# Pairs of rows in the layer-2 experts, a later channel-mix constant, a shorter router, and identity products in planned holes of a four-layer transformer kernel

## The chip, the core and the metric

The kernel runs on one core of a Trainium2 chip. The core has five engines with a queue each: TensorE (PE in the profile, its weight loads PEld), VectorE (DVE), ScalarE (ACT), GpSimd (POOL) and SyncE (SP, which here only issues DMAs). Every queue runs in program order; engines wait for each other through semaphores. The metric is the device time of one execution in microseconds; all tensors are float32.

## The reference, cut to what matters

Four "macaron" layers work on `x` of shape 4 rows (B) x 512 tokens (S) x 128 features (D). Each layer adds half a feed-forward, an attention, and half a feed-forward again, each on a layer norm of `x`:

```python
x = x + 0.5 * L0_ffn(ln(x));  x = x + L0_attn(ln(x));  x = x + 0.5 * L0_ffn(ln(x))
x = x + 0.5 * L1_ffn(ln(x));  x = x + L1_attn(ln(x));  x = x + 0.5 * L1_ffn(ln(x))
x = x + 0.5 * L2_ffn(ln(x));  x = x + L2_attn(ln(x));  x = x + 0.5 * L2_ffn(ln(x))
x = x + 0.5 * L3_ffn(ln(x));  x = x + L3_attn(ln(x));  x = x + 0.5 * L3_ffn(ln(x))
```

The parts that the change touches are these. The layer-2 feed-forward is a top-1 mixture of 8 experts, per row:

```python
gates = softmax(x @ Wg); expert = argmax(gates); gate = the chosen one's share
pos = running count of the row's tokens of this expert; keep if pos < 512 // 8
y[expert, pos] = gelu(x @ W1[expert]) @ W2[expert]      # W1: 128 x 512, W2: 512 x 128
out[token] = gate * y[expert, pos]                      # zero for tokens over capacity
```

The layer-3 feed-forward mixes each token with the one before it (`mu * x + (1 - mu) * x_prev`) ahead of three products. Layer 0's feed-forward is a top-2 mixture of 8 experts with a shared expert; layer 1's is a low-rank adapter (LoRA) with a gate; layer 1's attention is over the 4 rows at the same token, so row b needs rows 0 to b; the attentions of layers 2 and 3 are 16 heads of 8 features over the row's own tokens, causal in layer 2.

## The kernel before, in words

Layer 0 up to its second routing has an order of its own and is not touched. From the second layer-0 feed-forward to the end everything is one plan, made while the program is built. Each piece of work is a Python generator. It yields a request (`PE(0.95, "psum")`, `DVE(0.7)`, `any_of({...})`: an engine, or a choice of engines, with a cost in microseconds, and the buffers that it needs), and when the request is granted it records the instructions. `run` grants, again and again, the request that can start first; among those that start within `CLOSE` = 0.05 of it, it takes the lowest `RANK`. The table `RANK` holds one number for each process. The order in which requests are granted is the order of every engine's queue, SP's included, so the plan's costs set the order and the chip then runs that order at its own pace. `free` and `took` keep count of buffers in the plan; `clock.done` is the plan's time.

The processes, by name:

- `tile0` to `tile19` (`tiled`): the experts of layer 0's second feed-forward on 128-token tiles. L880 are the up products, L928 transposes, L940 the down products; the results go out by `sorted_y<-ys`.
- `first0` to `first3`: gathers of a row's results (`fetched`, L963 and L972), then the LoRA, attention and LoRA of layer 1 (`l1_row`: `lora`, `l1_attn`). L1364 scales `dT` by the LoRA's gate, which VectorE made (L1554); L1522 is the product after it.
- `heads` (`to_heads`): when all tiles are done it frees the tiles' weights, issues 23 DMAs on SP (L2511) for the weights of layers 2 and 3, calls `l3_others` (L2420: `nmu` = 1 - mu, one VectorE instruction, which reads the transfer issued fourth from the end, `l_mu`), and prepares the two value buffers `V` (L1838, one memset each on GpSimd).
- `send0` to `send7` (`l2_sent`): norm, router, slots of row n % 4 in the first (n < 4) and second mixture; the tokens are scattered to DRAM by four indirect DMAs on GpSimd (L2327).
- `take0` to `take7` (`l2_taken`): the row's 8 x 64 token slots are loaded as `X` (L2345, on SP), transposed (L2351), and go through the experts: 32 up products of 64 columns each (L2366), gelu, 32 down products in pairs that share the array (L2384), and a DMA back.
- `mix0` to `mix7` (`l2_added`): four gathers on GpSimd (L2409) and adds into `x`.
- `begin`, `turning`, `scoring` (L1931), `weighing` (L1947, the exponentials on ScalarE), `masking` (L1959), `values` (L1973), `turned` (L1994), `end`: the attentions of layers 2 and 3, eight "rows" k in order; `channels0` to `channels6`: layer 3's feed-forward; `half0`, `half1`: the last row's end in two halves.

PSUM has three `big` tiles (two banks each) and two `one` tiles in the plan.

Of the kernel before, what the change touches and what calls it, by code (L numbers as in the profile page):

```python
# [17 lines left out]
P = 128  # L18
# [3 lines left out]
NE = 8  # L22
# [18 lines left out]
def done(b):  # L41
# [9 lines left out]
CLOSE = 0.05  # L51
RANK = {
    "begin0": 7.13, "begin1": 16.87, "begin2": 2.08, "begin3": -4, "begin4": 2.25, "begin5": 16.3, "begin6": 18.65, "begin7": 5.19,
    "channels0": 2.52, "channels1": 8.5, "channels2": 0.21, "channels3": -14.23, "channels4": 27.64, "channels5": 35.57, "channels6": 55.73,
    "end0": -14.5, "end1": 16.73, "end2": 9.28, "end3": -13.76, "end4": 20.26, "end5": 8.69, "end6": 7.09, "fetching": 36.35, "first0": 12.23,
    "first1": 12.99, "first2": 13.46, "first3": 15.39, "half0": -16.36, "half1": -8.54, "kept0": 9.26, "looked": 68.09, "looked0": 55.15,
    "looked1": 38.53, "looked2": 55.16, "looked3": 44.23, "looked4": 53.01, "looked5": 64.26, "looked6": 56.59, "masking": 45.18, "mix0": 9.64,
    "mix1": 11.51, "mix2": 7.93, "mix3": -7.76, "mix4": 13.42, "mix5": 20.24, "mix6": 9.63, "mix7": 16.21, "placing": -4.73, "scoring": 23.21,
    "send0": -6.03, "send1": 10.23, "send2": 15.94, "send3": 6.71, "send4": 33.89, "send5": 9.79, "send6": 16.23, "send7": 37.79, "take0": -3.51,
    "take1": -6.11, "take2": 22.65, "take3": 5.52, "take4": 16.36, "take5": 23.51, "take6": 10.29, "take7": 21.36, "tile0": 8.75, "tile1": 6.94,  # L60
    "tile2": 4.64, "tile3": 9.21, "tile4": 1.92, "tile5": 9.1, "tile6": -2.3, "tile7": 4.99, "tile8": 9.81, "tile9": 10.06, "tile10": 10.38,
    "tile11": 10.39, "tile12": 11.4, "tile13": 11.41, "tile14": 11.42, "tile15": 10.69, "tile16": 12.44, "tile17": 12.45, "tile18": 12.46,
    "tile19": 12.87, "turning": 58.41, "values": 43.5, "weighing": 38.58, "whole_l2": 4.79, "whole_l3": 12.44,
}
FETCH = 4.0
DEARER = {"PE": 0.0, "ACT": 0, "DVE": 0.3, "POOL": 0.5, "SP": 0.0}
# [201 lines left out]
def program(ctx: ExitStack, tc: tile.TileContext, a: dict, out: bass.AP, worst):  # L268
# [193 lines left out]
    def by_expert(w, rooms, key):  # L462
# [385 lines left out]
        def tiled(work, iwho):  # L848
# [5 lines left out]
            def unit(u):  # L854
# [28 lines left out]
                yield PE(0.08 + 0.87 * n, "big")  # L883
# [9 lines left out]
                yield PE(0.08 + 0.87 * n, "big", at=t0)  # L893
# [3 lines left out]
                yield DVE(0.58 * n, "us", at=max(clock.done, t2))  # L897
# [15 lines left out]
                yield any_of({"DVE": 0.22 * n, "POOL": 0.1 + 0.35 * n}, at=t2)  # L913
# [498 lines left out]

    def run(procs, calm):

        busy_till = {e: 0.0 for e in ("PE", "DVE", "ACT", "POOL", "SP")}
        clock.on, clock.procs = True, procs
        while procs:
            able = []
            for p in list(procs):
# [30 lines left out]
                if t is not None:  # L1450
                    e = min(r.ways, key=lambda e: max(t, busy_till[e]) + r.ways[e] + DEARER[e])
                    able.append((max(t, busy_till[e]), p.rank, p, kind, e))
# [6 lines left out]
            us = p.req.ways[e]  # L1459
            clock.begun, clock.done, clock.kind, clock.engine = t, t + us + LATENCY, kind, e  # L1460
# [8 lines left out]
    def normal(b, make, kind, ones=False, half=False):  # L1469
# [20 lines left out]
        for h in range(2):  # L1490
            yield any_of({"ACT": 0.97, "DVE": 0.7}, *([kind] if h == 0 else []), at=t0)
            if h == 0:
                took(kind)
                xn = make()
                t1 = clock.done
            for t in (2 * h, 2 * h + 1):
                if clock.engine == "ACT":
                    nc.scalar.activation(xn[:, t, :], x[b][:, t, :], AF.Identity, bias=off[:, t : t + 1], scale=rs[:, t : t + 1])
                else:
                    nc.vector.tensor_scalar(xn[:, t, :], x[b][:, t, :], rs[:, t : t + 1], off[:, t : t + 1], ALU.mult, ALU.add)  # L1500
# [23 lines left out]
    def lora(b, w, work, wait=()):  # L1524
# [20 lines left out]
        yield DVE(0.65, at=t0)  # L1545
# [5 lines left out]
        yield DVE(0.5, at=max(clock.done, t1))  # L1551
# [279 lines left out]
    def heads_at_once(procs, rows, w, work, w3, late):  # L1831
# [5 lines left out]
        for t in V:  # L1837
            nc.gpsimd.memset(t, 1.0)  # L1838
        queries, keys, turns, inverse, through = {}, {}, {}, {}, {}
        sets, us, open_sets = {}, {}, [0, 0]  # L1840
# [33 lines left out]
        def begin(k):  # L1874
# [30 lines left out]
            yield moving(S, wait=[f"valued{k - 2}"] if k > 1 else [])  # L1905
# [3 lines left out]
        def turning():  # L1909
            for k in range(len(rows)):  # L1910
                for g in range(NG):
                    yield any_of({"DVE": 0.46, "ACT": 0.6, "POOL": 0.8}, "qkq", wait=f"q{k}", at=0.0)
                    took("qkq")
                    t = work.tile([P, S], F32, tag="qkq", name="qkq", bufs=2)
                    scaled(t, queries[k], turn[:, g : g + 1])
                    turns[k, g] = t
                    happened(f"turn{k}.{g}")
                    if g == NG - 1:
                        free("q")

        def scoring():
            for i, (k, g, parts, ends) in enumerate(todo):
                yield PE(0.15 + 0.87 * width(parts) / 512, "big", "big", wait=[f"begin{k}", f"turn{k}.{g}"], at=0.0)
# [15 lines left out]
        def weighing():  # L1939
            for i, (k, g, parts, ends) in enumerate(todo):  # L1940
                n = width(parts)
                us[i] = []
                for h in range(NJ // 2):
                    yield ACT(0.1 + 0.87 * n / 512, "pT", wait=f"S{i}", at=0.0)
                    took("pT")
                    p = work.tile([P, 2, S], F32, tag="pT", name="pT", bufs=6)
                    nc.scalar.activation(p[:, :, :n], sets[i][h][:, :, :n], AF.Exp, scale=scale)  # L1947
                    free("big")
                    us[i].append(p)
                    happened(f"E{i}.{h}")  # L1950
# [11 lines left out]
        def values():  # L1962
            po = None
            for i, (k, g, parts, ends) in enumerate(todo):
                first = po is None
                yield PE(0.15 + 0.87 * width(parts) / 512, *(["one"] if first else []), wait=[f"{'M' if rows[k][2] else 'E'}{i}.{h}" for h in range(NJ // 2)], at=0.0)
# [298 lines left out]
    def l2_mixed(w, work, b, rooms, key, late):  # L2265

        sent, kept = [], []
        return l2_sent(w, work, b, rooms, key, sent, kept), l2_taken(w, work, b, rooms, sent, late), l2_added(work, b, rooms, kept, late)

    def l2_sent(w, work, b, rooms, key, sent, kept):  # L2270
# [17 lines left out]
        yield ACT(0.24)  # L2288
        nc.scalar.activation(sh, sh, AF.Exp)
        m, order = little([P, NT, NE], "chosen"), little([P, NT, NE], "order")  # L2290
        gate, best = little([P, NT], "gates"), little([P, NT], "best")
        sofar = little([P, NT - 1, NE], "sofar")
        yield DVE(1.0)
        nc.vector.tensor_reduce(sm, sh, AX.X, ALU.add)
        nc.vector.reciprocal(sm, sm)
        nc.vector.tensor_tensor(sh, sh, wide(sm, NT), ALU.mult)
        nc.vector.tensor_reduce(best, sh, AX.X, ALU.max)
        nc.vector.tensor_scalar(gate, best, 0.5, None, ALU.mult)
        yield DVE(1.4)
        nc.vector.tensor_tensor(order, sh, wide(best, NT), ALU.is_equal)  # L2300
        nc.vector.tensor_tensor(order, order, w["c_first"].unsqueeze(1).to_broadcast([P, NT, NE]), ALU.mult)
# [5 lines left out]
        yield PE(0.5, "psum")  # L2307
        pp, k = spare()
        before = pp[:, : NT * NE].rearrange("p (t e) -> p t e", t=NT)
        l2_counts(before, m, sofar, w)  # L2310
        islot = little([P, NT], "islot", mybir.dt.int32)
        at, place, slot = little([P, NT, NE], "at"), little([P, NT], "place"), little([P, NT], "slot")
        kept += [gate, islot]
        yield DVE(1.4)
# [3 lines left out]
        nc.vector.tensor_tensor(at, m, w["c_slot0"].unsqueeze(1).to_broadcast([P, NT, NE]), ALU.mult)  # L2318
        nc.vector.tensor_reduce(slot, at, AX.X, ALU.add)
# [15 lines left out]
    def l2_taken(w, get, b, rooms, sent, late):  # L2335
# [3 lines left out]
        NH = HID // P  # L2339
        none = NE * CAP  # L2340
        kx, kh, n = ("Xl", "hl", 2) if late else ("X", "h", 1)
        yield ask("PE", 0.0, kx)
        took(kx)
        X = work.tile([P, NT, D], F32, tag="X", name="X", bufs=2 * n)
# [10 lines left out]
        XT = work.tile([P, NE, CAP], F32, tag="X", name="XT", bufs=2 * n)  # L2355
# [4 lines left out]
        for q in range(NE // 2):  # L2360
# [8 lines left out]
            h = work.tile([P, 2, NH, CAP], F32, tag="hr", name="hr", bufs=n * NE // 2)  # L2369
# [4 lines left out]
        yield ACT(2.6 + 2.6)  # L2374
# [3 lines left out]
        for q2 in range(2):  # L2378
# [9 lines left out]
            if q2 == 0:  # L2388
                took(kx)
                y = work.tile([P, NE // 2, D], F32, tag="X", name="y", bufs=2 * n)  # L2390
# [3 lines left out]
        free(kx, clock.done + 2.5)  # L2394

# [27 lines left out]
    def l3_ffn(b, w, get, last, halves=1):  # L2423
# [7 lines left out]
        for m in (1, 0):  # L2431
            yield DVE(1.2, f"t{m}")
# [208 lines left out]
    for kind, n in (("xn", 3), ("X", 2), ("h", 4), ("yg", 4), ("Xl", 4), ("hl", 8), ("ygl", 4), ("cx", 2), ("t0", 1), ("t1", 1), ("kT3", 1), ("r3", 1)):  # L2641
# [17 lines left out]

    def to_heads():  # L2660
# [8 lines left out]
        l3_others(w3, pools[-1])  # L2669
# [3 lines left out]
        yield POOL(3.7)  # L2673
        idle[0] = heads_at_once(procs, rows, wa, work, w3, late)
        for b in range(B):
            procs.append(process(f"channels{b}", l3_ffn(b, w3, late, False), 10 + B + b, [f"mix{B + b}", "change"]))
# [9 lines left out]
    def mixture(n, b, after):  # L2686
        first = n < B
        send, take, add = l2_mixed(w2, (lambda: pools[1]) if first else late, b, row_rooms[b], f"slots{n}", not first)
        procs.append(process(f"send{n}", send, 10 + n, [after]))
        k = n - 1 if first else n - 2  # L2690
        procs.append(process(f"take{n}", take, 10 + n, [f"send{n}", "fetching", "heads"] + ([f"take{k}"] if k >= 0 else []) + ([] if first else ["change"])))
        procs.append(process(f"mix{n}", add, 10 + n, [f"take{n}"] + ([f"mix{n - 1}"] if n else [])))

    for b in range(B):
        mixture(b, b, f"first{b}")
        mixture(B + b, b, f"end{b}")
# [33 lines left out]
```

## Time and profile before

| | us |
|---|---|
| three timed runs, median | 1293.74 |
| lowest, highest of them | 1288.74, 1293.77 |
| the profiled execution, its own time | 1290.51 |
| the profiled execution, its span from first to last instruction | 1288.7 |

| engine | busy us in the span | share |
|---|---|---|
| PE | 1158.0 | 90% |
| DVE | 891.8 | 69% |
| ACT | 707.1 | 55% |
| PEld | 614.1 | 48% |
| POOL | 341.4 | 26% |

The mean granted TensorE clock is 0.958. In the profile's rows a float32 product shows as two matmul records; a transpose by the identity shows as one. A line of a group or of the timeline names the engine, the source line, the tile written and the tile read, and in brackets the idle time of the engine before it and who ended it. "x16" is the number of records merged into one line.

### The profile page before, as it was taken

What the parts mean: (1) busy time and instruction counts of PE and PEld (TensorE: products, weight loads), DVE (VectorE), ACT (ScalarE), POOL (GpSimd) and SP (SyncE); (2) the same over time, 40 slices, a digit from 0 to 9 for tenths busy, and PEclk for the clock granted to TensorE, in tenths of its full rate; (3) what the DMA queues carried; (4) which work ended last, traced back from release to release, by engine and by line L of the source; (5) the groups of instructions that cost most, each with busy time, mean ns of one, the idle gap of its engine ahead of it and who ended that gap; (6) DMA issues with size and microseconds to landing.
All of it is one profiled execution on the core that took longest, in us unless ns stands there. A gap on an engine that the chain in (4) does not pass through costs nothing.

```text
span 1288.7 us, 20383 instructions
## 1 busy us (share of the span) xinstructions
PE 1158.0 (90%) x7066; PEld 614.1 (48%) x7066; DVE 891.8 (69%) x2342; ACT 707.1 (55%) x1030; POOL 341.4 (26%) x323
## 2 busy tenths in 40 slices
PE   5899989999989999997998848798998999999994
PEld 3455544334425335364555426474675665443332
DVE  5697777988988998769668737876637655344233
ACT  2435545654644635442444424466777778778882
POOL 4430223022310400202134535623325233111010
PEclk9899989999999999998999958898999999999998
DMA  8123312111111111101321130001100010000000
GB/s 308 35 72 90 89 57 68 66 60 40 60 62 50 66 50 49 51 1 48 117 66 48 34 109 25 20 16 34 35 25 27 16 34 18 17 25 2 9 9 11
DMA packets 63490, 65.02 MB, mean 50 GB/s; under 512 B 11538, under 2 KB 53907, under 8 KB 62867
## 3 DMA queue, kind: packets, MB, share of 16 engines
q1 hardware_dynamic: 57236, 51.04, 11.8%
q0 software_dynamic: 6144, 12.60, 3.3%
q8 instruction: 59, 0.97, 0.3%
q14 instruction: 51, 0.42, 0.1%
HBM read 29.13 MB, written 17.69 MB: 36 GB/s over the span
## 4 chain that ended last, share of the span: by engine, by line
PE 62%; DVE 18%; issue 8%; DMA 4%; POOL 3%; ACT 3%; SPq 1%; POOLq 0%; DVEq 0%; ACTq 0%
PE big L1931 8%; PE one L1973 7%; PE big L1200 6%; PE one L1214 6%; PE one L2366 4%; PE big L880 3%; PE big L758 3%; PE one L1243 2%; PE one L1522 2%; PE big L603 2%; DMA yg<-sorted_y,ito 2%; DVE sums L1209 2%; PE one L2384 2%; PE big L1150 1%; PE one L1994 1%
## 5 line engine op out<-in xcount | busy, mean ns | idle before, releaser
L1947 ACT ACTIVATE pT<-big 128x1024 f32<-128x1024 f32 (+1 forms) x224 | 205.9, 964 | 43.5 <-PE big L1931 36.7
L1201 ACT ACTIVATE pT<-big 128x1024 f32<-128x1024 f32 x128 | 125.7, 1034 | 54.9 <-PE big L1200 52.8
L1200 PE MATMUL big<-qk 64*128 64x512 f32 x512 | 126.6, 605 | 6.8 <-DVE U L1236 6.8
L1931 PE MATMUL big<-qkq,qkk 32*128 32x512 f32 (+3 forms) x1024 | 127.3, 553 | 1.2 <-ACT pT L1947 1.0
L1214 PE MATMUL one<-pT,V 128*64 128x512 f32 x512 | 116.9, 598 | 0.0
L1973 PE MATMUL one<-pT,V 128*32 128x512 f32 (+3 forms) x1024 | 112.1, 526 | 0.9 <-DVE own L1537 0.6
L583 POOL DMA_INDIRECT sorted_x<-xn,irows x64 | 72.5, 1133 | 69.6 <-DVE share L555 22.4
L1485 POOL TENSOR_TENSOR rs<-rs,root 128x4 f32<-128x4 f32 x35 | 37.4, 1068 | 170.3 <-DVE rs L1483 116.0
L1209 DVE TENSOR_TENSOR sums<-sums,pT 128x1024 f32<-128x1024 f32 x64 | 78.1, 1220 | 5.1 <-ACT qk L1152 0.5
L1200 PEld LDWEIGHTS big<-qk 64*128 64x128 f32 x512 | 46.3, 186 | 69.0 <-issue 40.3
L880 PE MATMUL big<-w_w,xsT 128*128 x156 | 75.3, 614 | 1.8 <-ACT xsT L1352 1.2
L1931 PEld LDWEIGHTS big<-qkq,qkk 32*128 32x128 f32 x1024 | 46.6, 183 | 58.7 <-issue 39.5
L758 PE MATMUL big<-w_w,xsT 128*128 x156 | 73.5, 594 | 0.3 <-issue 0.3
L1291 ACT COPY U<-one 128x512 f32<-128x512 f32 x32 | 18.8, 587 | 94.9 <-PE one L1214 92.8
L839 POOL DMA_INDIRECT yg<-sorted_y,ito x32 | 38.4, 1200 | 122.4 <-DMA sorted_y<-ys 61.5
L1214 PEld LDWEIGHTS one<-pT,V 128*64 128x64 f32 x512 | 33.9, 136 | 77.1 <-issue 72.4
L603 PE MATMUL big<-xnT,w_w 128*128 128x512 f32 x128 | 61.2, 614 | 6.9 <-DVE u L608 5.8
L1959 DVE TENSOR_TENSOR pT<-pT,w_c_tri 128x256 f32<-128x256 f32 (+1 forms) x96 | 48.1, 524 | 21.0 <-ACT pT L1947 20.7
L2366 PEld LDWEIGHTS one<-XT,w_l_w 128*128 128x128 f32 x464 | 54.1, 192 | 12.4 <-ACT hr L1352 4.8
L2366 PE MATMUL one<-XT,w_l_w 128*128 128x64 f32 x464 | 57.2, 276 | 0.7 <-DVE x L350 0.3
L2409 POOL DMA_INDIRECT yg<-row_y,islot x32 | 34.2, 1070 | 75.5 <-DMA row_y<-y 67.9
L605 ACT ACTIVATE t<-big,w_bs 128x512 f32<-128x512 f32 x32 | 21.7, 685 | 56.0 <-PE big L603 33.7
(435 smaller groups left out, 2333.6 us busy)
## 6 DMA issues: line engine op xcount, KB each, us to landing
other<-qk SPq DMA_DIRECT2D x64, 256.0 KB, 2.3
xs<-sorted_x SPq DMA_DIRECT2D x78, 64.0 KB, 1.8
sorted_y<-ys SPq DMA_DIRECT2D x38, 128.0 KB, 1.8
w_w<-in_w SPq DMA_DIRECT2D x2, 2048.0 KB, 13.6
w_l_w<-in_l_w SPq DMA_DIRECT2D x8, 256.0 KB, 3.0
w_l_w<-in_l_w SPq DMA_DIRECT2D x1, 2048.0 KB, 7.7
X<-row_x SPq DMA_DIRECT2D x8, 256.0 KB, 2.8
row_y<-y SPq DMA_DIRECT2D x8, 256.0 KB, 2.3
```

Of the source, the lines that this page charges most:

```text
L583: apart(nc.gpsimd.indirect_dma_start(out=sorted_x[:, :], out_offset=bass.IndirectOffsetOnAxis(ap=irows[:, b, j, t : t + 1], axis=0), in_=x ...
L603: nc.tensor.matmul(pa[:, m, :], lhsT=w["w13"][:, NE, m, odd, c * P : (c + 1) * P], rhs=xTs[b], start=True, stop=True)
L758: nc.tensor.matmul(pa[:, k, :], lhsT=st[u]["xT"][:, k * P : (k + 1) * P], rhs=w["w13"][:, bass.ds(st[u]["e"][k], 1), m].rearrange("p o a b ...
L880: nc.tensor.matmul(pa[:, k, :], lhsT=xT[:, k * P : (k + 1) * P], rhs=w["w13"][:, bass.ds(e[k], 1), m].rearrange("p o a b -> p (o a b)"), s ...
L1200: nc.tensor.matmul(sT[:, u, :], lhsT=k[r, t * P : (t + 1) * P], rhs=q[r, :], start=True, stop=True)
L1201: nc.scalar.activation(pT[:, :, t % 2, :], sT, AF.Exp, scale=scale)
L1209: nc.vector.tensor_tensor(s, s, pT[:, :, m, :], ALU.add)
L1214: nc.tensor.matmul(po[r, :], lhsT=V[:, t, :], rhs=pT[:, u, t % 2, :], start=(t == 0), stop=(t == NT - 1), tile_position=(0, 64 * u))
L1931: nc.tensor.matmul(sT[j // 2][:, j % 2, c : c + n], lhsT=keys[k][r, t * P : (t + 1) * P], rhs=turns[k, g][r, S - n :], start=True, stop=True)
L1947: nc.scalar.activation(p[:, :, :n], sets[i][h][:, :, :n], AF.Exp, scale=scale)
L1973: nc.tensor.matmul(po[32 * j : 32 * j + 32, S - n :], lhsT=V[k % 2][:, t, NJ * g + j, :], rhs=us[i][j // 2][:, j % 2, c : c + n], start=(t ...
L2366: nc.tensor.matmul(ph[:, j, c, :], lhsT=w["l2_w1"][:, 2 * q + j, c * P : (c + 1) * P], rhs=XT[:, 2 * q + j, :], start=True, stop=True)
```

## The change

- Rows 2 and 3 of the first mixture, and rows 0 and 1, 2 and 3 of the second (`PAIRS = (2, 4, 6)` names each pair's first) are taken through the experts two at a time by a new function, `l2_taken2`. It loads both `X`, and makes for each expert one product per 128 hidden features with 128 columns (64 of each row). Its down products use 128 columns of the array. Rows 0 and 1 of the first mixture are still taken alone. A pair's take starts when both rows have been sent, and both `mix` wait for it.
- `l3_others` becomes a process of its own, `others`, that waits for the planned arrival of layer 3's weights; so do the two memsets of `V` (`ones0`, `ones1`), with a cost in the plan.
- The router finds the argmax from the logits less their maximum, and not from the shares; the exponential and the gate (1 over twice the sum) stand beside the slots' arithmetic.
- `run` calls `kept_warm` before each request that it grants on TensorE. Where the plan leaves TensorE idle, and all `big` or all `one` tiles are free, it records products of the identity with itself (128 columns) into one of them, as many as fit at 0.23 each, and ends 0.2 before the next request.
- Some planned costs are raised or lowered, scaling of the queries (`turning`) is no longer offered to GpSimd, and all of `RANK` is new, so the order of the instructions is new from the second layer-0 experts on.

In the built program the changed kernel has 136 products of the identity: 10 ahead of the second plan of the tiles (the two one-row products `who`), 5 among the tiles, 56 between the last tile and the first score of layer 2's attention, 46 between that and the last score, and 19 after it. The order of all instructions up to the first 10 is as before.

```diff
+WARM = 0.23
 RANK = {
...
 }
+PAIRS = (2, 4, 6)
...
+    def kept_warm(t):
+
+        for kind, n, make in (("big", 3, big), ("one", 2, one)):
+            a = when(kind, n)
+            n = 0 if a is None else int((t - 0.2 - max(a, clock.busy["PE"] + LATENCY)) / WARM)
+            if n > 0:
+                took(kind)
+                junk = make() if kind == "one" else make()[:, 0, :]
+                for _ in range(n):
+                    nc.tensor.matmul(junk[:, :P], lhsT=ident, rhs=ident, start=True, stop=True)
+                free(kind, t - 0.2)
+                return
...
+            if e == "PE":
+                kept_warm(t)
...
-        for t in V:
-            nc.gpsimd.memset(t, 1.0)
+        def ones_in(m):
+            yield POOL(1.9)
+            nc.gpsimd.memset(V[m], 1.0)
...
-                    yield any_of({"DVE": 0.46, "ACT": 0.6, "POOL": 0.8}, "qkq", wait=f"q{k}", at=0.0)
+                    yield any_of({"DVE": 0.49, "ACT": 0.72}, "qkq", wait=f"q{k}", at=0.0)
...
-        yield ACT(0.24)
-        nc.scalar.activation(sh, sh, AF.Exp)
...
-        nc.vector.tensor_tensor(sh, sh, wide(sm, NT), ALU.mult)
-        nc.vector.tensor_reduce(best, sh, AX.X, ALU.max)
-        nc.vector.tensor_scalar(gate, best, 0.5, None, ALU.mult)
-        yield DVE(1.4)
-        nc.vector.tensor_tensor(order, sh, wide(best, NT), ALU.is_equal)
-        nc.vector.tensor_tensor(order, order, w["c_first"].unsqueeze(1).to_broadcast([P, NT, NE]), ALU.mult)
+        yield DVE(1.1)
+        nc.vector.scalar_tensor_tensor(order, sh, 0.0, w["c_first"].unsqueeze(1).to_broadcast([P, NT, NE]), ALU.is_equal, ALU.mult)
...
+    def l2_taken2(w, get, both):
...
+        for rooms, sent in both:
+            yield ask("SP", 0.05, "Xl")
...
+            ld = nc.sync.dma_start(out=X[-1], in_=rooms[0][:none, :].rearrange("(q p) d -> p q d", p=P)).ins
...
+        for e in range(NE):
+            yield PE(0.96, "psum", at=t0)
+            ph, k = spare()
+            for c in range(NH):
+                nc.tensor.matmul(ph[:, c * P : (c + 1) * P], lhsT=w["l2_w1"][:, e, c * P : (c + 1) * P], rhs=XT[:, e].rearrange("p i c -> p (i c)"), start=True, stop=True)
...
+        for q in range(2):
+            yield PE(3.7, "psum", at=gone[q])
+            py, k = spare()
+            for e in range(4):
+                for c in range(NH):
+                    nc.tensor.matmul(py[:, e * D : (e + 1) * D], lhsT=hs[4 * q + e][:, c, :], rhs=w["l2_w2"][:, 4 * q + e, c, :], start=(c == 0), stop=(c == NH - 1))
...
+    def others(w3):
+        yield DVE(0.2)
+        l3_others(w3, pools[0])
...
-        l3_others(w3, pools[-1])
...
-        yield POOL(3.7)
+        procs.append(process("others", others(w3), 9.0, ["loaded_l3"]))
```

## The prediction

> **What bounds the kernel now.** The page came first: TensorE is busy for 90% of the span, VectorE for 69%, and the second row of digits shows where TensorE ran at reduced clock.
>
> ```profile
> span 1288.7 us, 20383 instructions
> PE   5899989999989999997998848798998999999994
> PEclk9899989999999999998999958898999999999998
> ```
>
> The dip is slices 22 to 26. A table by stage, cut at the events named below, says what each stage lacks (columns: length, PE, PEld, DVE, ACT, POOL busy, clock, DMA share, GB/s):
>
> ```profile
> 597.30:741.00 143.70, 121.78 (x504) 71.82 (x504) 107.38 (x287) 62.43 (x118) 44.71 (x45) 0.93 0.23 64
> 741.00:837.60 96.60, 64.31 (x352) 46.91 (x350) 63.44 (x248) 33.49 (x80) 48.78 (x45) 0.75 0.17 51
> 837.60:1000.00 162.40, 151.73 (x1511) 101.26 (x1512) 104.79 (x366) 115.86 (x177) 56.30 (x51) 0.98 0.09 28
> 1000.00:1261.60 261.60, 259.73 (x2102) 122.76 (x2098) 119.44 (x385) 206.47 (x265) 50.17 (x44) 1.00 0.05 16
> 1261.60:1288.70 27.10, 8.38 (x44) 5.96 (x42) 10.86 (x40) 3.52 (x9) 1.45 (x2) 0.78 0.05 13
> ```
>
> Up to 597 nothing changes. 597 to 741 are layer 0's tiles; 741 to 837.6 is the way to the first score of layer 2, where TensorE is idle for 32.3 us and works 29.5 us at clock 0.50 (about 14.7 lost); from 837.6 to 1261.6 TensorE is idle for 12.6 in 424 us: here work on TensorE is time. ScalarE has 322 of these 424, near enough to matter if TensorE loses much. The last 27 us are the tail. The waits name the largest hole, and the timeline shows its cause:
>
> ```profile
> PE one L1522 <- ACT dT L1364: 17.4, 3, 14.7
> DVE nmu L2420 <- DMA w_l_mu<-in_l_mu: 16.8, 1, 16.8
> ...
> 741.58 0.37 SPq L2511 DMA_DIRECT2D w_l_w<-in_l_w  x1
> 755.87 0.43 SPq L2511 DMA_DIRECT2D w_l3f_wv<-in_l3f_wv  x1
> 784.07 0.38 SPq L2345 DMA_DIRECT2D X<-row_x  x1
> ```
>
> VectorE stands 16.8 us at `nmu` until mu has landed; the LoRA's gate is queued behind it, ScalarE's `dT` waits for the gate, TensorE for `dT`, 14.71 us. SP needs 14.7 us (741.6 to 756.3) to issue the 23 weights; the first `X` goes out long after.
>
> **The change part by part.** *The late `nmu`.* It now stands 77 rows further down VectorE's queue than the first tokens' slots, after the bias of layer 2 is ready; mu has landed by then. The 14.7 us go. What is late next: `send0` now stands ahead of the last tiles, so row 0's `X` (L2345's successor) is ready early, but on SP it is queued behind the 23 weights, and TensorE's queue has `X`'s transposes right after 17 identity products and 8 products of layer 1. `X` thus lands 14.7 (weights) + 0.4 (issue) + 2.8 (landing, median of eight) + 0.5 = 18.4 us after the tiles' last store. Everything behind on TensorE (layer 1's output product, row 0's experts, the next LoRA) waits, and those who need it. So one 15 us stall is exchanged for another, about 13 us long; but it now lies before row 0's experts, not before its router.
>
> *Order.* I priced each queue's new order with the old rows' durations. Ahead of the tiles' last down product stand 7 us more of TensorE work and 8 us more of VectorE work (which is 75% busy there): +7 us, end at 748 instead of 741. Between it and the first score TensorE has 28 us instead of 44; of the 16, 7 went ahead and 9 behind the first score.
>
> First score: 748 + 18.4 = 766.5 for `X`, against 787.6 before. From `X` to the first score it was 50.0 us; the same chain (experts, gelu, store, four gathers, norm, projections) with less at half clock takes about 48: **815 instead of 837.7, so -23**.
>
> *Pairs.* Here a rule speaks against the change, so row and rule are weighed:
>
> ```profile
> 851.34 2.00 PE L2366 MATMUL one<-XT,w_l_w 128*128 128x64 f32 x16
> 859.76 3.79 PE L1685 MATMUL one<-w_c_ident,pv 128*128 128x128 f32 x32
> 801.62 1.97 PE L2384 MATMUL big<-w_l_w,hr 128*64 128x128 f32 x32
> ```
>
> Eight 64-column products take 1.93 us to the next row (1.73 where L2366 follows in another place), 0.22 to 0.24 each; sixteen 128-column ones take 3.62, 0.226 each. The Trainium skill (TensorE: Matmul & The Clock Gate, "Back-to-back issue gap") has the gap grow with the columns, N / 2.4 + 2.5 ns: by it two products of 64 cost what one of 128 does, and pairing gains nothing. By the rows 64 cost as much as 128. The rows decide: a pair had 64 products at about 0.228, 14.6 us, and has 32 at 0.226, 7.2: about 7 us, **-21 for three pairs** (0 by the rule). Down products: before 4 x 1.9 = 7.6 a pair, now 32 x 0.226 = 7.2: 0. Gelu and moves out of PSUM keep their sizes; the two stores carry the same bytes: 0, as TensorE covers them. A pair waits for its later row: `send3` stands about 24 us of TensorE work behind `send2`; the attentions of rows 0 and 1 (about 20 us of scores and values each) and layer 1's rest cover it, and where they end a hole opens (next).
>
> *Identity products.* 136 x 0.226 = 31 us that TensorE must now work through. In a hole they cost 0, without one up to 31. 10 lie in the 4.39 us before `who` (2.3 us at full clock), 56 are in the holes before the first score (inside the 48 and the `X` stall), 19 in the tail's waits: 0. The 46 in the attention tell where the order expects TensorE to stand: 39 of them around the downs of the first pair, 9 us in one place. With the 0.2 to 0.4 left after each run and waits that the plan does not see I put 20 us of holes where before had 12.6: **+7**. What they win is clock. The same page ("Why this matters for your kernels") lets the clock fall after gaps over about 3 us; the trace shows 0.50 from 706.6 after a gap of 2.21 us and from 809.0 after 1.95, while 1.70 at 677 did nothing. By the rule only runs for holes over 3 us (85 of the products) can win, by the trace those near 2 us also. Work at half clock after 597 lost 23.8 us in all; most lay where the chain waited anyway. I take -2 after the first score and -1.5 in the tail (bounds 0 and -8).
>
> *Shorter router.* Each row loses four small VectorE instructions net and one of 0.6 us, about 1 us, and ScalarE's exponential leaves the chain (0.2 and two hops): 1.4 us a row. For row 0 the SP queue hides it, for the others TensorE's full queue: 0; without cover -1.4 on each of the rows that a hole waits for, at most -5.
>
> *Memsets, `turning`.* The two memsets (1.80 us each) stand together now; beside one of them VectorE's L1536 took 1.64 us instead of 0.18, so VectorE may stand still 3 us; the `X` stall covers it. Nine scalings leave GpSimd (1.73 each) for VectorE or ScalarE (0.5 to 0.7), which have slack: 0, or +3.
>
> **Sum.** After the first score: 451.1 - 21 + 9 + 7 - 2 - 1.5 = 443. 815 + 443 = 1258 of span; the profiled run's own time was 1.8 above its span, the median of three 3.2 above the profiled run. I say **1262** for the median.
>
> **The rivals.** *The plan holds (0.2).* The weights do not keep `X` back, or the chain from `X` is shorter: TensorE has only 28 us of products and 39 identities (9 us) there, so the first score could come at 795 to 800: 1242. For it: that queue is short. Against it: SP needed 14.7 us for these transfers. *Half the gain lost again (0.13).* From the first score ScalarE is at 85% and the exponentials take 1.02 us twice for each 2.1 us of scores and values; if they set the pace in layer 3, the last pair's 7 us, the 9 us moved and some holes come on top: 1280. *Not slower, not faster (0.05)*: both of these mishaps, about 1293. *Slower (0.07).* TensorE starves between the attention of rows 0 and 1 and the first pair. That pair waits for row 3, whose whole layer 1 is behind the `X` stall; then begin2 needs store, gathers and norm, which took 24 us from the last down product to the next transposes (806.5 to 830.6). If row 3's slots are later than the attention of rows 0 and 1 by 30 us, the hole is 20 + 30 and the order of rows leaves nothing to fill it: 1300. Below 25 us late it is still a gain. Against it: in the order 16 us of TensorE work stand between row 3's router and its `X`, and the slots, scatter and load took 12 us before (775.3 to 787.6). *The likeliest (0.55)* is the sum, 1250 to 1276.
>
> **How the numbers follow.** 0.5% (6.5 us) is about what a measurement of this kernel can tell from no change. Faster by more: 0.55 + 0.2 + 0.13 = 0.88; within: 0.05; slower: 0.07. The range leaves out 2 in 10, mostly the slow cases and the edge of the best: 1238 to 1286.
>
> **What would show it.** Right: no wait at `nmu`; a wait of TensorE for `X<-row_x` of 10 us or more just after the tiles; first score near 815; paired up products at 0.9 us for four; a hole near the first pair filled with identity records; clock near 0.97. Wrong: first score before 800 (the SP queue is no wall) or after 830; TensorE idle for over 40 us between the first and last score; ScalarE, not TensorE, ending the waits of layer 3; up products of the pair slower than 0.3 us each.

## The result and the profile after

| | us |
|---|---|
| before, median of 20 runs | 1293.49 |
| changed, median of 20 runs (lowest, highest) | 1284.18 (1278.54, 1290.61) |
| ratio, 95% interval | 0.9932 (0.9918 to 0.9946) |
| changed, the profiled execution: its own time, its span | 1288.94, 1287.2 |

Ratios, here and below, are of the runs that lie within 1.5% of the fastest run of the same kernel. The change saves 9.3 us, 0.7%, where 31 were forecast. The page of the changed kernel, the span and the rows of TensorE and its clock:

```profile
span 1287.2 us, 20162 instructions
...
PE   5899989999999999988899949989999999999995
...
PEclk9899989999999999989899987899999999999998
```

The dip of the clock is narrower than before (mean 0.965, was 0.958); the digit 4 in slice 24 (740 to 772 us) is a hole that was not there. The table by stage of the same execution, cut at the same events (columns as before):

```profile
601.70:752.20 150.50, 132.10 (x579) 78.43 (x579) 115.59 (x323) 67.83 (x131) 49.01 (x52) 0.97 0.21 59
752.20:823.20 71.00, 53.98 (x359) 47.42 (x357) 38.16 (x158) 23.90 (x54) 36.07 (x34) 0.78 0.25 73
823.20:1259.70 436.50, 419.68 (x3378) 227.08 (x3377) 244.97 (x792) 319.83 (x437) 101.52 (x95) 0.99 0.07 20
1259.70:1287.20 27.50, 11.89 (x80) 9.43 (x80) 10.77 (x40) 3.51 (x9) 1.42 (x2) 0.77 0.05 13
```

This execution reached the tiles at 601.7 where the one of before had 597.3, with the same instructions up to there. Its clock stood at 0.50 for 27.3 us there, for 20.5 before. Those 4.4 us are not put down to the change; as a whole, this execution lies 4.8 above the median of its kernel. Counted from the tiles on, the stages are:

| stage | before | forecast | changed |
|---|---|---|---|
| tiles | 143.7 | 150.7 | 150.5 |
| tiles' end to first score | 96.6 | 67 | 71.0 |
| first to last score, and values | 424.0 | 443 with the tail | 436.5 |
| tail | 27.1 | | 27.5 |

So the forecast held up to the first score, within 4 us. Behind it 443 were forecast and 464.0 came (462.9 in a second profile of the same kernel, set 2 below). That is 21 of the 25 us that are missing (1258 of span forecast; 1287.2 less the 4.4 of the common part is 1282.8).

The hole of slice 24 is the wait for `X`, as forecast, and SP's queue shows why. The changed kernel's timeline, SP's lines around the last weights:

```profile
753.11 0.74 SPq L2603 DMA_DIRECT2D w_l_w<-in_l_w  x1
...
768.04 0.43 SPq L2603 DMA_DIRECT2D w_l3f_wv<-in_l3f_wv  x1
768.70 0.38 SPq L2372 DMA_DIRECT2D X<-row_x  x1
```

and its waits, TensorE's longest behind the tiles:

```profile
PE one L2378 <- DMA X<-row_x: 13.8, 1, 13.8
```

`nmu` has no wait any more. The scatter of row 0 was issued from 749.2 to 754.3; `X` stood behind 15.6 us of weight issues. The longest planned hole behind the first score is beside the first pair (timeline of the changed kernel; L1425 is the identity product, two records each; L2475 the pair's down products, L2442 its transposes):

```profile
947.68 1.06 PE L1425 MATMUL big<-w_c_ident 128*128 128x128 f32 x8
948.57 3.74 PE L2475 MATMUL one<-w_l_w,hr 128*128 128x128 f32 x32
952.14 5.52 PE L1425 MATMUL big<-w_c_ident 128*128 128x128 f32 x48
958.12 0.63 PE L2442 MATMUL one<-w_c_ident,X 128*128 128x128 f32 x4 [0.45 <-DMA X<-row_x]
958.92 0.63 PE L2442 MATMUL one<-w_c_ident,X 128*128 128x128 f32 x4 [0.18 <-DMA X<-row_x]
959.38 0.61 PE L1425 MATMUL big<-w_c_ident 128*128 128x128 f32 x4
```

24 identity products fill 5.5 us, and then TensorE still waits 0.45 for the transfer. So the hole is real and the filling covers it; left empty, in a run below, it is a wait of 5.86 us for the same transfer.

The ledger of the stage from first to last score compares before with changed, and adds up to the 12.5 us by which the stage grew (a record's busy time is counted up to the next record of TensorE): up products 52.3 to 30.5, so -21.7; layer 1's work that now lies here +13.2 (the largest: `pv` 4.8, `wqkv` 3.4, `xns` 1.5); identity products +11.8; idle 12.6 to 16.8, +4.3; scores and values +2.7; many small ones +2.2. The clock is inside these sums: TensorE worked 10.0 us of the stage at half clock, 4.3 before, which is 2.8 us of the 12.5; 1.7 of them are in `pv`.

### The profile page after: what moved, and what is told of

Same layout as the page of the kernel before. It is cut to its first block, busy times and chain, and to the rows that moved or that the text cites. A ratio compares the mean times of both kernels' runs of the same rounds, so it can differ in the third digit from the quotient of the medians.

```text
span 1287.2 us, 20162 instructions
## 1 busy us (share of the span) xinstructions
PE 1174.3 (91%) x6954; PEld 630.3 (49%) x6954; DVE 895.4 (70%) x2328; ACT 700.6 (54%) x1015; POOL 328.1 (25%) x320
## 4 chain that ended last, share of the span: by engine, by line
PE 63%; DVE 21%; issue 5%; DMA 3%; ACT 3%; POOL 2%; SPq 1%; DVEq 0%; POOLq 0%; ACTq 0%
PE big L1956 8%; PE one L1998 8%; PE big L1203 5%; PE one L1217 5%; PE big L761 4%; PE one L1541 3%; PE big L883 3%; PE one L1246 2%; PE big L606 2%; DVE sums L1212 2%; PE big L1153 2%; PE one L2475 1%; PE one L2019 1%; PE big L635 1%; PE one L794 1%
## 5 line engine op out<-in xcount | busy, mean ns | idle before, releaser
L1956 PE MATMUL big<-qkq,qkk 32*128 32x512 f32 (+3 forms) x1024 | 130.9, 555 | 0.1
L1504 POOL TENSOR_TENSOR rs<-rs,root 128x4 f32<-128x4 f32 x35 | 37.1, 1059 | 226.8 <-DVE rs L1502 183.5
L1956 PEld LDWEIGHTS big<-qkq,qkk 32*128 32x128 f32 x1024 | 49.2, 184 | 61.8 <-issue 40.8
L353 DVE TENSOR_TENSOR x<-x,one 128x512 f32<-128x512 f32 x31 | 21.2, 684 | 57.2 <-PE one L1541 33.1
L1984 DVE TENSOR_TENSOR pT<-pT,w_c_tri 128x256 f32<-128x256 f32 (+1 forms) x96 | 52.4, 563 | 2.5 <-ACT pT L1972 2.2
L608 ACT ACTIVATE t<-big,w_bs 128x512 f32<-128x512 f32 x32 | 21.7, 685 | 56.5 <-PE big L606 30.9
L322 POOL TENSOR_TENSOR rs<-rs,root 128x4 f32<-128x4 f32 x16 | 20.7, 1298 | 118.7 <-DVE rs L321 118.6
L1998 PEld LDWEIGHTS one<-pT,V 128*32 128x32 f32 x1024 | 23.9, 108 | 54.6 <-issue 37.9
```

The source lines that it names most:

```text
L1956: nc.tensor.matmul(sT[j // 2][:, j % 2, c : c + n], lhsT=keys[k][r, t * P : (t + 1) * P], rhs=turns[k, g][r, S - n :], start=True, stop=True)
L1984: nc.vector.tensor_tensor(d, d, w["c_tri"].unsqueeze(1).unsqueeze(1).to_broadcast([P, 2, len(parts), P]), ALU.min)
L1998: nc.tensor.matmul(po[32 * j : 32 * j + 32, S - n :], lhsT=V[k % 2][:, t, NJ * g + j, :], rhs=us[i][j // 2][:, j % 2, c : c + n], start=(t ...
```

## The experiments

There were five sets; each set ran on one chip, together with the kernel before. Chips differ: the kernel before took 1293.5 in sets 2 and 5, and 1320.6, 1316.3 and 1314.4 in sets 1, 3 and 4. Times are compared inside a set, and ratios to before, with care, across sets of like chips.

**Set 1. No identity products** (`kept_warm` returns at once).

> The changed kernel without any identity product; the order of everything else is as in the changed kernel. Theory A (the holes they were planned for are partly not there on the chip, so they are work): between first and last score TensorE loses 11.8 us of identity products and gains at most 4 us of idle time; the median falls from 1284 to 1272-1280. Theory B (they sit in real holes and keep the clock): the holes come back as idle time at the same length, half-clock stretches are added, the median is 1284-1294 and the stage between first and last score is 436 us or longer.

Measured 1307.17, ratio 0.9901 (0.9874 to 0.9928). The changed kernel did not run on this chip; on the like chips of sets 3 and 4 it had 0.9857 (0.9824 to 0.9890) and 0.9874 (0.9839 to 0.9909). Leaving them out won nothing; idle time between first and last score was 32 us without any.

**Two of 64 columns for one of 128** in the pairs (the edit, shortened).

```
-  matmul(ph[:, c*P:(c+1)*P], lhsT=w1[:, e, ...], rhs=XT[:, e] (128 columns))
+  for i in range(2):
+      matmul(ph[:, c*P+i*CAP : ...], lhsT=w1[:, e, ...], rhs=XT[:, e, i, :])
```

> The changed kernel with each pair's up product of 128 columns issued as two of 64 columns, 96 products more and nothing else moved. If 64 columns cost what 128 cost (0.226 us), 96 x 0.226 = 21.7 us more TensorE work, all after the first score: the median goes from 1284 to 1302-1306, less where a pair's up products stand beside a hole. If the gap grows with the columns (two of 64 cost one of 128), the median stays at 1284-1286, and pairing itself brought nothing.

Measured 1328.38, ratio 1.0030 (1.0009 to 1.0052), against 0.9857 and 0.9874 on the like chips: about 21 to 23 us of 1320, where 21.7 were expected if 64 columns cost what 128 cost.

**Row 0's `X` ahead of the weights** (`to_heads` keeps its 23 transfers back; `l2_taken` issues them right behind its own load of `X`).

> The changed kernel with row 0's X issued on SP ahead of the 23 weight transfers, not behind them; order on all other queues as before. X can then go out when the scatter has landed (about 756.5 on the profiled run's time) and lands near 759.5 and not 771.5. If the SP wall is on the path to the end, the first score comes 10-12 us earlier and the median is 1272-1276. Rival: the next late thing (row 3's layer 1, the weights that are now late by one wait, layer 2's gathers) gives it back before the end: the wait at X goes, the first score comes under 5 us earlier or the holes after it grow, median 1280-1285.

Measured 1288.76, ratio 0.9753 (0.9726 to 0.9780), against 0.9857 and 0.9874 on the like chips; repeated in sets 3 and 5.

**The kernel before with mu first.**

```
+  behind.insert(0, behind.pop(-4))     # l_mu
   brought(behind)
```

> The kernel before with one DMA moved: mu is issued first of the 23 weight transfers, not fourth from the end. If VectorE's 16.8 us at nmu were on the path, that wait falls to about 3 us and the median from 1293.5 to 1281-1284, which is all that the whole change brought. Rival (it would be exchanged for another wait, since SP stays busy with weights until 756 and X comes behind it): under 4 us gained, 1290-1294.

Measured 1306.43, ratio 0.9889 (0.9863 to 0.9916): 14.2 us for one moved DMA. Its timeline at `nmu` and its stage up to the first score:

```profile
751.88 0.38 SPq L2511 DMA_DIRECT2D w_l_mu<-in_l_mu  x1
753.69 0.17 DVE L2420 TENSOR_SCALAR nmu<-w_l_mu 128x2 f32<-128x2 f32 x1 [2.74 <-DMA w_l_mu<-in_l_mu]
```

```profile
751.10:832.20 81.10, 62.61 (x356) 46.31 (x354) 63.06 (x248) 33.69 (x80) 48.85 (x45) 0.81 0.21 61
```

16.8 us of wait became 2.7, and the stage 81.1 us instead of the 96.6 of the first chip. So the stall was on the path. Removing it alone is worth most of what the whole change wins on like chips (1.1% against 1.3 and 1.4).

**Set 2. The changed kernel again.**

> The changed kernel unaltered, beside the kernel before, on the chip of this set: the reference for the variants, since the four runs before showed a kernel before that takes 1320 and not 1293. If chips only scale, the ratio is 0.993 again (about 1311). If it is under 0.99, leaving the identity products out (0.990) won nothing or lost.

Measured 1279.74, ratio 0.9914 (0.9879 to 0.9948). A second profile of the same kernel, on a chip like the first; the stages up to the first score and behind it:

```profile
749.00:812.90 63.90, 46.98 (x358) 40.64 (x356) 38.37 (x157) 23.64 (x54) 35.21 (x33) 0.87 0.27 81
812.90:1248.50 435.60, 417.02 (x3378) 224.60 (x3377) 245.19 (x793) 319.72 (x437) 102.00 (x96) 1.00 0.07 20
```

Behind the first score it agrees with the first profile. Ahead of it, it is 7 us shorter: around the same 14 us wait for `X` the clock stood at 0.50 for 13.7 us here and for 27.3 there. In this stage TensorE worked 7.3 us at half clock here and 21.9 there, and half of the difference is about the 7 us. The Trainium skill (TensorE: Matmul & The Clock Gate, "What's actually happening") has the clock decided in free-running windows of 3413 ns; these stretches are 4 and 8 of them. It is the largest difference between the two executions.

**Single rows** (`PAIRS = ()`).

> The changed kernel with no pairs: every row goes through the experts alone, as in the kernel before; the order is planned anew and is that of the changed kernel up to the first score. TensorE has about 21.5 us more up products after the first score, but the plan sees few holes there: 5 identity products and not 46, and the first pair's wait for row 3 is gone. Theory A (pairing opens holes of about 15 us, so its net gain is a third of its arithmetic): 4-9 us slower than the changed kernel of the same set. Theory B (the pairs' whole 21 us are won): 18-24 us slower. Theory C (the wait eats all): equal or faster.

Measured 1300.48, ratio 1.0055 (1.0037 to 1.0072): 20.7 us slower than the changed kernel of the set, as theory B had it. From first to last score:

```profile
817.10:1268.80 451.70, 428.56 (x3676) 234.80 (x3675) 246.03 (x792) 323.73 (x446) 105.04 (x96) 1.00 0.07 19
```

23.1 us of it are idle (451.7 - 428.56) and 1.2 identity products, where before had 12.6 idle. There are no pairs here. So the new order makes most of the new holes, not the pairs. The pairs add some: the changed kernel of this set has 30 us of idle time and identity products. In the profiles this stage is only 16.1 us longer than with pairs (up products 20.9 more, holes 6 less); ahead of the first score, where the two kernels have one order, this execution was 6 us longer, with the clock at 0.50 for 34 us and not 14.

**`X` first, no identity products.**

> Row 0's X ahead of the weights, and no identity products. With X early the longest hole, for which the clock fell, is gone. If identity products are work where holes are small: 5-10 us faster than with them (ratio 0.968-0.972 against 0.975). If they keep the clock up in the holes around the first pair and the first score: slower than with them, 0.977-0.985.

Measured 1274.25, ratio 0.9854 (0.9820 to 0.9887). It lies just above the range of "slower", but the 0.975 it was to be held against came from another chip; set 5 settles it.

**The kernel before with identity products.**

> The kernel before with the identity products alone (87 of them, in the holes that its own plan sees; order otherwise as before). They stand beside stalls that are longer than planned (the 14.7 us before dT). If they only keep the clock: half-clock time between the tiles and the first score falls from 48 us to about 30, 3-8 us faster (0.994-0.998). If the chain there waits anyway: no change, 0.998-1.003.

The built kernel has 91 of them. Measured 1289.69, ratio 0.9972 (0.9958 to 0.9987): 4 us faster. Its stage up to the first score:

```profile
742.20:836.30 94.10, 68.70 (x452) 56.37 (x451) 64.17 (x249) 33.76 (x80) 48.94 (x45) 0.84 0.17 53
```

Half-clock time there went from 48 to 29 us, as forecast. Most of what it saved is waiting again: 94.1 us instead of 96.6.

**Set 3. The changed kernel, a third time.**

> The changed kernel unaltered, the reference of this set: ratio to before 0.990-0.995, stage from first to last score 434-437 us with about 30 us of identity products and idle time.

Measured 1298.26, ratio 0.9857 (0.9824 to 0.9890), better than the 0.990 to 0.995 expected; from first to last score it took 447.4 us, not 434 to 437, 22.9 of them idle. On this chip the clock was at 0.50 for 17 us in that stage; in the first profile for 10.

**The last pair alone** (`PAIRS = (6,)`).

> The changed kernel with only the last pair (rows 2 and 3 of the second mixture) taken together; the four other rows of the first two pairs alone. The order is the same up to the first score; after it the plan records 2 identity products and not 46. TensorE has 2 x 7.2 = 14.4 us more up products than with three pairs. Theory A (the first two pairs pay for their arithmetic with the holes in which they wait for their later row, measured 17 us more holes than before): within 5 us of three pairs. Theory B (holes would be there anyway, in other places): 11-15 us slower than three pairs, and 6-8 us faster than single rows.

Measured 1308.64, ratio 0.9938 (0.9920 to 0.9955): 10.4 us slower than three pairs, nearer to theory B. From first to last score, three pairs and then one:

```profile
829.60:1277.00 447.40, 424.53 (x3377) 228.11 (x3378) 243.19 (x792) 320.13 (x437) 101.78 (x95) 0.98 0.07 19
```

```profile
815.90:1273.60 457.70, 432.08 (x3548) 230.72 (x3547) 247.07 (x795) 322.88 (x441) 103.75 (x96) 0.98 0.07 19
```

Idle 25.6 and 1.3 of identity products here, 22.9 and 11.8 with three: the first two pairs open about 8 us of holes. In time they still win 10 of their 14.4 us. By the profiles up products and holes give 7 of these 10; scores and values, the same work in both kernels, were 4 us shorter with three pairs, which is not put down to them. The order behind the first score was planned anew here, so pairs and order are not told apart.

**`X` first, again.**

> Row 0's X ahead of the 23 weights, with identity products, on the chip of this set beside the changed kernel. From the tiles' end to the first score 51-53 us instead of 64-71. If the first score's lead reaches the end: 11-16 us faster than the changed kernel, ratio to before near 0.982. If it is lost in later waits: under 5 us.

Measured 1282.69, ratio 0.9748 (0.9719 to 0.9778), 15.6 us faster than the changed kernel of the set. SP's first lines and the stage up to the first score:

```profile
758.06 0.36 SPq L2374 DMA_DIRECT2D X<-row_x  x1
758.47 0.50 SPq L2378 DMA_DIRECT2D w_l_w<-in_l_w  x1
```

```profile
754.80:805.80 51.00, 46.57 (x362) 40.16 (x361) 36.55 (x158) 23.93 (x54) 34.35 (x32) 0.93 0.33 101
```

51.0 us instead of 71.7; behind it 446.8 against 447.4. The lead reaches the end whole. Part of the 20.7 is that the profiled run of the changed kernel lay 8 us above its median; between the medians the lead is 15.6.

**No identity products behind the first score.**

> The changed kernel without the 65 identity products behind the first score (46 before the last score, 19 in the tail); the 71 before it stay, order unchanged. Theory A (they are work that TensorE must do beside little real idle time): the stage between first and last score falls from 436 to 426-431, 5-10 us faster. Theory B (they fill holes that are there, since without any of them idle time there was 26-32 us): idle time returns to about 27 us, half-clock stretches of 10-20 us come back, the same or up to 8 us slower.

Measured 1298.01 against 1298.26: no difference. From first to last score:

```profile
821.80:1270.50 448.70, 417.44 (x3285) 221.15 (x3284) 243.16 (x793) 320.28 (x437) 102.80 (x96) 0.97 0.07 19
```

448.7 - 417.4 = 31.3 us idle: what the products fill comes back as idle time (22.9 + 11.8 with them). Half-clock time rose from 17 to 31 us, and the busy time of all other products by 4.7. Theory A, that they are surplus work, falls.

**Set 4. Why are there holes?** The reference, the changed kernel:

> The changed kernel unaltered, the reference of this set. From first to last score 435 us on a chip whose kernel before takes 1293, 447 on one where it takes 1316; TensorE waits there for VectorE 10-12 us in 16-17 places.

1297.80, ratio 0.9874. Then without the causal masks:

> The changed kernel without the causal masks: the 64 minimum instructions on VectorE (L1984, about 24.7 us of them in the first 100 us after the first score) are left out, so later tokens are attended to as well; the order of everything else is the same. Theory D (layer 1's remaining work that now lies behind the first score shares VectorE with the masks, 80% busy there against 69% before, and TensorE's waits for VectorE are its price): the waits of TensorE for VectorE behind the first score fall from 10-12 us to 5 or less, and that stage is 5-9 us shorter than in the changed kernel. Rival (each wait is the length of a short chain, product to VectorE to product, with nothing queued ahead): the waits stay at 9 us or more, the stage is under 4 us shorter.

1293.92, ratio 0.9828 (0.9797 to 0.9859; reference 0.9839 to 0.9909, so the intervals overlap). The stage, first with masks, then without:

```profile
822.40:1268.90 446.50, 421.60 (x3378) 225.57 (x3378) 243.44 (x793) 320.11 (x437) 102.44 (x96) 0.99 0.07 19
```

```profile
827.70:1268.30 440.60, 420.16 (x3377) 225.04 (x3377) 201.88 (x696) 319.77 (x437) 100.71 (x95) 0.99 0.07 20
```

5.9 us shorter with 42 us less VectorE work, as theory D had it; but TensorE's waits for VectorE fell only from 12.4 to 9.0 us, as its rival had it. And the control:

> The kernel before without its causal masks (the same minimum instructions, L1959, left out; order the same), the control for the run without masks of the changed kernel. Theory D: little to win, since TensorE waits for VectorE only 6 us there: the stage from first to last score is 0-4 us shorter. If it is shortened as much as in the changed kernel, the masks explain nothing of the difference.

1325.36, ratio 1.0092 (1.0062 to 1.0121): slower with less work. In that profile the clock is at 0.50 for 37 us between first and last score. Why, was not followed further, so the control says nothing on masks. With the masks a quarter of TensorE's waits for VectorE went. The other 202 us of VectorE's work stayed, so no run shows how much of the rest its load explains.

**Set 5. What are the identity products worth once `X` is first?**

> Row 0's X first and all 136 identity products, beside the two variants below on one chip. Where the kernel before takes 1294: ratio 0.980-0.984 (1268-1273); where it takes 1314 or more: 0.974-0.976.

> Row 0's X first, no identity products. If identity products win by the clock even where no long hole is left: 4-10 us slower than with all of them, with 20 us more half-clock time behind the tiles. If they are neutral (as the run without those behind the first score had it): within 3 us.

> Row 0's X first, identity products only ahead of the first score (71 of 136). If those behind it are neutral here too: within 3 us of all of them. If they cost TensorE time: 3-8 us faster. If they hold the clock: 3-8 us slower.

| `X` first, with | us | ratio |
|---|---|---|
| all 136 identity products | 1266.78 | 0.9802 (0.9783 to 0.9822) |
| the 71 ahead of the first score | 1273.02 | 0.9844 (0.9828 to 0.9860) |
| none | 1276.76 | 0.9867 (0.9847 to 0.9886) |

Here they win 10 us. 6 of them are those behind the first score, clear of noise; the other 4 are not (the last two intervals overlap). The stage from first to last score with all, and with none:

```profile
799.10:1235.00 435.90, 418.28 (x3377) 224.75 (x3377) 245.55 (x793) 319.64 (x437) 102.30 (x96) 0.99 0.07 20
```

```profile
807.20:1247.80 440.60, 415.10 (x3284) 221.82 (x3284) 244.45 (x792) 319.52 (x437) 101.44 (x95) 0.97 0.07 19
```

With none, 25.5 us are idle and the clock is at 0.50 for 24 us; with all, 17.6 and 6.8. The version with `X` first and all products beats the kernel before by 27 us on this chip, and the changed kernel by about 16 in set 3.

Without products the holes can be read. Of these 25.5 us TensorE waits 13.8 for VectorE in 19 places, 5.9 for one `X`, 3.6 for ScalarE and 1.7 for GpSimd; in the kernel before it was 6.2 for VectorE in 11 places, 4.0 for one `X`, and 1.8 for ScalarE. So over half of the 13 us of new holes are waits for VectorE. The long hole stands beside the first pair here too (L2481 are its down products, L2448 its transposes):

```profile
928.18 8.73 PE L2481 MATMUL one<-w_l_w,hr 128*128 128x128 f32 x64
942.77 1.97 PE L2448 MATMUL one<-w_c_ident,X 128*128 128x128 f32 x8 [5.86 <-DMA X<-row_x]
```

and a wait of that kind in the kernel before, from first to last score:

```profile
PE one L2351 <- DMA X<-row_x: 4.0, 1, 4.0
```

## Why the prediction was wrong, point by point

Up to the first score the mechanism was right and the sizes were within 4 us. The step that failed is the sum behind the first score, and in it above all the term for holes, +7: the runs showed +16. Three smaller terms were off too. The measured 1284.18 still lies within 1238 to 1286, but the gain is under a third of the one forecast, and none of the signs of being wrong came (first score at 818.8; 16.8 us idle; 0.224 us a product): none of them watched idle time and filling together.

- **`nmu` exchanged for the weights' queue: right, and the price too.** 14 us of stall forecast gone, 13 come; 14.2 us is what moving mu alone wins in the kernel before, 15.6 what moving `X` alone wins in the changed one. The two all but cancel.
- **Tiles +7, `X` 18.4 us after the tiles: right** (150.5; 19.4 to the first transpose).
- **First score 815: 818.8** with the common part taken off, 812.3 in the second profile. The earlier score was a gain only as far as work had not moved behind it.
- **Pairs -21: right** (up products -21.7). The eight products from 934.63 to 936.42 take 0.224 each; single rows and split columns cost 21 to 23 us in time. That two of 64 cost one of 128 does not hold for these products. The prediction set the page against the rows too sharply: the same section of the Trainium skill (TensorE: Matmul & The Clock Gate, "Back-to-back issue gap") says that its formula is for an isolated product, and that at few columns it counts too little, as it leaves out the weight load. What sets the 0.22 us here, no run showed.
- **Moved work +9: 13.** The priced order named layer 1's rest, at prices taken from another place. 4 us, of which 1.7 are `pv` at half clock.
- **Holes +7: this step failed.** I put 20 us of idle and identity time where before had 12.6, as if the planned holes took the place of the unplanned. They came on top: 11.8 + 16.8 = 28.6. Single rows have about 12 us more than before without any pair, so the order makes most of them; against one pair, three pairs have 8 more. The products themselves are not the cost, since without them the idle time returns (31.3 us and 25.5): the holes are. 9 us.
- **Clock behind the first score -2, tail -1.5: neither came.** Before had only 6.8 us at half clock there, so that little was to be won; the changed kernel had 10.2 (3.4 in the second profile). The tail is 27.5 for 27.1. 4 us.
- **Not in the sum:** scores and values 2.7 us longer on the same shapes, which is unexplained, and 2.2 in small groups, of which 1.6 are the `wos` products and the transposes of `U`: 2.7 us of these ran at half clock, none before.

4 + 9 + 4 + 5, less 0.7 for the pairs, is the 21 that were missing behind the first score. The rival "half the gain lost again" (1280) is nearest in time, but ScalarE is not its cause. The prediction put ScalarE at 85% from the first score; its own table has 322 us of 424, 76%. Behind the first score TensorE waits 3.5 us for ScalarE in nine places (1.8 in six before) and 10.3 for VectorE in sixteen (6.2 in eleven before). VectorE has more to do there, as layer 1's moved attention now stands beside the masks. The first 100 us after the first score, before:

```profile
837.60:937.60 100.00, 93.18 (x902) 62.71 (x906) 68.54 (x246) 69.78 (x108) 34.38 (x32) 0.97 0.10 29
```

and changed:

```profile
823.20:923.20 100.00, 91.41 (x815) 58.16 (x818) 79.67 (x266) 65.95 (x104) 36.26 (x33) 0.97 0.06 19
```

80% instead of 69%, and waits of a kind that before did not have there (the changed kernel's waits in this window):

```profile
PE one L1704 <- POOL pv L1697: 1.1, 1, 1.1
PE one L1998 <- DVE kv L1357: 0.8, 1, 0.8
PE one L1620 <- DVE kv L1357: 0.8, 1, 0.8
PE one L2393 <- DVE kv L1357: 0.8, 1, 0.8
```

In the last three the next product on TensorE, of whatever line, starts when VectorE has copied layer 1's `kv` out of PSUM. VectorE was not behind there. It stood idle until TensorE's product had ended, 5.7 us ahead of the four such copies of `q` and `kv`, as in:

```profile
845.07 0.29 DVE L1357 COPY q<-one 128x128 f32<-128x128 f32 x1 [0.48 <-PE one L1620]
845.28 0.41 DVE L1357 COPY kv<-one 128x256 f32<-128x256 f32 x1
845.84 1.97 PE L2393 MATMUL one<-XT,w_l_w 128*128 128x64 f32 x16 [0.81 <-DVE kv L1357]
```

So these 2.4 us are short turns from TensorE to VectorE and back, and not VectorE's load. That such turns make most of the other waits too fits the run without masks; no run showed it, and it stays open.

The "slower" rival's hole of 50 us, a first pair that starves, is the one at 952: 6 us long.

## What to carry to other kernels

An earlier milestone is not yet a gain: write the ledger of the bounding engine from the change to the end (work, idle, filling), and let what leaves one stage enter the next. Here the holes that the plan filled were added to those that it did not see. When one wait is removed, look at what the same queue holds back next: here one DMA at the head of SP's queue was worth 14 us before the change, and another one 15 after it.

## What had not been expected of the hardware

- The same kernel takes 1293 us on some chips and 1314 to 1321 on others. In the kernel before with mu first, on a 1320 chip, TensorE was busy 425.9 us from first to last score and at half clock for 30.7; before, on a 1293 chip, 411.5 and 6.8, for the same products. The clock is lower on such chips in every set: the mean granted clock of the kernel before was 0.947, 0.946 and 0.948 in sets 1, 3 and 4, and 0.958 and 0.959 in sets 2 and 5. The changed kernel gains more there (ratios 0.986 and 0.987 against 0.993 and 0.991). Why chips differ, no run shows.
- Identity products won 10 us with `X` first, on a 1293 chip. Without them the clock fell for 10 us at 941, in the hole of 5.86 us. Short holes count too: in the changed kernel it fell for 3.4 us at 831.0 after a hole of 1.06 us, and at 878.8 after one of 0.8, where the prediction had looked to those near 2 us.
- Taking VectorE's masks out of the kernel before made it 11 us slower, for a reason that was not found.
